# Two-layer convolution and attention kernel: the filters' stream pauses until its PSUM bank is copied out, and one column product is copied by VectorE

## The chip, the core and the metric

The kernel runs on one core of a Trainium2 chip. The metric is the time of one execution on the device in microseconds; lower is better. The engines are named as the profile names them: PE is TensorE (matmuls; PEld are its weight loads), DVE is VectorE, ACT is ScalarE, POOL is GpSimd, SP is SyncE, which here only issues DMAs. All data are fp32; an fp32 matmul appears in the trace as two records, so "x4" records of one product are two matmuls.

## The reference

The input x is 4 images of 256 channels and 48 x 48 pixels. Two layers follow each other, each added to its input. The first is a 3x3 convolution with batch norm, relu and self-attention with 8 heads; the second predicts, for each pixel, softmax weights for five 3x3 filters of growing dilation, applies them, mixes the six results with a 1x1 convolution, and normalizes over the batch.

```python
def layer0(g):                      # g = group norm of x, 32 groups
    h = relu(batch_norm(conv3x3(g, conv_w) + conv_b))
    q, k, v = qkv_w @ h + qkv_b     # 8 heads of 32 channels, 2304 pixels
    attn = softmax(q.T @ k * 32 ** -0.5)
    return proj_w @ (v @ attn.T) + proj_b

def layer1(g):                      # g = group norm of x + layer0
    guidance = conv3x3(g, W_cat)    # 45 channels = 5 filters x 9 taps
    outs = [g]
    for i, d in enumerate((1, 6, 12, 24, 36)):
        w = softmax(guidance[:, 9 * i : 9 * (i + 1)], axis=1)
        outs.append(sum_over_taps(shift(g, tap * d) * w[:, tap]))
    y = conv1x1(concat(outs), W_scale)
    return batch_norm_over_the_batch(y) * gamma + beta

x = x + layer0(group_norm(x))
x = x + layer1(group_norm(x))
```

## The kernel before

**Stages.** The images go through in a pipeline. Attention of image b runs alone (the function `attention`). Between two attentions lies a joint stage: the convolution and the q, k, v products of image b (`conv_qkv`, and in it `conv_blocks` for images 1 to 3) run together with the second layer of image b-1 (`dynamic_filters`). There are three joint stages, for `dynamic_filters` of b = 0, 1 and 2; a fourth and last run of `dynamic_filters` (b = 3, called `alone` in the code) has no convolution beside it. In the code, `b < B - 2` with B = 4 therefore means the first two joint stages.

**How the order is made.** Every engine executes its instructions in the order in which the program emits them. That order is worked out while the kernel is built, by a small planner. `clock` holds a planned time for PE, DVE, ACT and POOL; `clock(engine, ns, after)` puts a piece of work on an engine's planned time. `dynamic_filters` consists of streams, Python generators: `loads` (the DMAs of the far weights), `far` (the four large dilations, as matmuls), `rest` (sums for the next image's convolution), `near` (the dilation 1), `filters` (the softmax weights) and `mixes` (the 1x1 convolution). A stream yields the planned time at which its next piece may be emitted, either as a number or as a function that is asked again. The function `drive` looks through the streams in that order, and the first whose time has come (not later than PE's planned time) emits its piece. Only where none is due does `drive` take a step of the other generator, the convolution and qkv, and that only if `need[0]` says that its inputs and its PSUM bank are free in the plan. If nothing is due at all, PE's planned time is moved on. When the streams are done, `run(1e9)` emits what is left of the other generator.

**The softmax weights.** `weights(cs)` makes the weights of one chunk or of a pair of chunks; a chunk is a sixth of the image, 384 columns. `filters` calls it for the sets (0,), (1,), (2, 3), (4, 5), and asks before each that its first chunk be at most two beyond the chunk that `mixes` is at. In `weights`, PE computes `pg` (line 1545; 36 records for one chunk, 72 for a pair), ACT and DVE copy it to `lg` (1555, 1556), PE transposes it to `pt`, DVE and ACT make the softmax in `e1`, PE transposes it back to `pw` (1599), ACT copies `pw` to `lg` (1603), and SP stores `lg` to `w_d` in DRAM (1606). `pg`, `pt` and `pw` are all made by `misc`, which hands out the same PSUM bank each time: the next `pg` must wait until `pw` has been copied. The far weights `wq` are read back from `w_d` (1635) and meet PE in `wT` (1723); the near weights `ws` are read from it too (1802).

**The convolution of the joint stages.** `conv_blocks` works through 12 tiles, `t` from 0 to 11: six combinations of input rows, in the order 1, 2, 3, 4, 0, 5, with two halves of the output channels each. A tile consists of four column products, n = 0 to 3, of 288 columns each (`pc`, line 1176), which go round through two PSUM banks. The product n = 0 is copied to `one` (1191), the product n = 1 is combined with `one` into the two sums `two` (1201 and 1202), and the products 2 and 3 are added to them (1212 and 1214). Where the plan finds DVE late (`busy_dve`), ACT copies the products first (1196, 1207) and DVE or POOL adds.

**The start of a joint stage.** The last chunk of image b-1 is projected, its group norm is finished, and its 2 x 1152 columns in two halves of the image are normalized, half h = 0 of the channels by DVE (648) and h = 1 by ACT (2114). Between these pieces `run` emits convolution steps by their planned length: `run(2500)` and `run(1000)` during the norm's statistics, `run(1900)` after the first half of the image is normalized, `run(1400)` after the second. Tile t = 1 begins there: its n = 0 copy is emitted between the two halves of the normalization.

Of the kernel before, what the change touches and what calls it, by code (L numbers as in the profile page):

```python
# [15 lines left out]
B, C, HH, WW = 4, 256, 48, 48  # L16
# [42 lines left out]
def conv_preact_kernel(  # L59
# [12 lines left out]
    nc = tc.nc  # L72
# [480 lines left out]
    with tc.tile_pool(name="w", bufs=1) as wpool, tc.tile_pool(  # L553
# [60 lines left out]
        one = wpool.tile([P, 1], F32, tag="one", name="one")  # L614
# [20 lines left out]
        for j in range(2):  # L635
            t = act.tile([P, NH, PADW * PADW], F32, tag=f"pad{j}", name=f"pad{j}")
            t = t.rearrange("p h (r w) -> p h r w", w=PADW)
# [6 lines left out]
        def rows_of(t):  # L644
            return t.rearrange("p (r w) -> p r w", w=WW)
# [96 lines left out]
        clock = Clock()  # L742
        free = {}

        def slot(tag, bufs):

            ends = free.setdefault(tag, [])
            return ends[-bufs] if len(ends) >= bufs else 0.0
# [238 lines left out]
        class Blocks:  # L987
# [81 lines left out]
            def axpy(self, out, x, a, y):  # L1069
                if len(x.shape) == 4:  # L1070
                    for h in range(NH):
                        self.axpy(out[:, h], x[:, h], a, y[:, h])
                    return
                nc.vector.scalar_tensor_tensor(
                    out=out, in0=x, scalar=a, in1=y, op0=ALU.mult, op1=ALU.add
                )
# [31 lines left out]
        def conv_blocks(b, psum_tile, blocks, pool, hid):  # L1108

            axpy = blocks.axpy  # L1110
            tt = nc.vector.tensor_tensor
            rows = hid.rearrange("p h (t r w) -> p h t r w", r=4, w=WW)
            spare = list(blocks.spare)

            results, last = [], [0.0]

            def busy_dve():
                return clock.t["DVE"] > max(clock.t["ACT"], clock.t["PE"]) + 500

            def relu(o, r, y, end):  # L1120
                results.append((o, r, y, end))

            def relus(limit):
                while results and results[0][3] + 150 <= limit:
                    o, r, y, end = results.pop(0)
                    nc.scalar.activation(  # L1126
                        rows[:, o, :, r, :], rows_of(y), AF.Relu,
                        bias=bn_t[:, o : o + 1], scale=bn_s12[:, o : o + 1],
                    )
                    clock("ACT", 660, end)  # L1130

            def before(i, o):

                s12, d12, s34, d34 = (blocks.held[:, j, o] for j in range(4))
                if i == 0:
                    t = spare.pop(0)
                    axpy(t, s34, -4.0, s12)
                    relu(o, 2, t, clock.both(800))
                    either(s12, s12, s34, ALU.subtract)
                elif i == 5:  # L1140
                    t = spare.pop(0)
                    axpy(t, d34, -2.0, d12)
                    relu(o, 1, t, clock.both(800))
                    axpy(d12, d34, -8.0, d12)
                    clock.both(800)

            def target(i, o):

                if i in (1, 3):
                    return blocks.first[o]  # L1150
                if i in (2, 4):
                    return blocks.held[:, 1 if i == 2 else 3, o]
                return spare.pop(0)

            def after(i, o, y):

                s12, d12, s34, d34 = (blocks.held[:, j, o] for j in range(4))
                if i in (2, 4):
                    s, d = (s12, d12) if i == 2 else (s34, d34)
                    either(s, y, blocks.first[o], ALU.add)  # L1160
                    either(d, blocks.first[o], y, ALU.subtract)
                elif i in (0, 5):
                    relu(o, i and 3, y, either(y, y, s12 if i == 0 else d12, ALU.add))

            blocks.scaled()
            need[0] = lambda: 150 + max(slot("c", 2), blocks.end[STEPS[0]])
            for t, (i, o) in enumerate(TILES):
                u = us.pop(t)
                y = target(i, o).rearrange("p (n s) -> p n s", s=2)
                for n, j in enumerate((1, 2, 0, 3)):  # L1170
                    m = psum_tile(f"pc_{b}_{i}_{o}_{j}")[:, :XN]
                    clock("PE", 0, slot("c", 2), blocks.end[i, j])
                    z = blocks.of[i].rearrange("p (j h n) -> p j h n", j=4, h=NH)[:, j]
                    relus(max(clock.t["ACT"], clock.t["PE"]))
                    for h in range(NH):
                        nc.tensor.matmul(
                            m, u[:, h, j], z[:, h], start=(h == 0), stop=(h == NH - 1)
                        )
                        clock("PE", MM * XN / CH)
                        if h == 0:  # L1180
                            need[0] = lambda: 0.0
                            if t == 1 and n == 3:
                                blocks.along(ORDER[1])
                            if n == 0:
                                if t + 2 < len(TILES):
                                    us[t + 2] = taken(t + 2)
                                before(i, o)
                            yield MM * XN / CH
                    if n == 0:
                        one = pool.tile([P, XN], F32, tag="one", name=f"one_{b}_{i}_{o}")  # L1190
                        nc.scalar.copy(one, m)
                        end = clock("ACT", 400, clock.t["PE"])
                    elif n == 1:
                        two = pool.tile([P, 2, XN], F32, tag="two", name=f"two_{b}_{i}_{o}")
                        if busy_dve():
                            nc.scalar.copy(two[:, 1], m)
                            end = clock("ACT", 400, clock.t["PE"])
                            either(two[:, 0], one, two[:, 1], ALU.add, end)
                            either(two[:, 1], one, two[:, 1], ALU.subtract, end)
                        else:  # L1200
                            tt(two[:, 0], m, one, ALU.add)
                            tt(two[:, 1], one, m, ALU.subtract)
                            end = clock("DVE", 900, clock.t["PE"], end)
                    else:
                        to = y[:, :, n - 2]
                        if busy_dve():
                            nc.scalar.mul(to, m, 1.0 if j == 0 else -1.0)
                            end = clock("ACT", 450, clock.t["PE"])
                            either(to, to, two[:, n - 2], ALU.add, end)
                        else:  # L1210
                            if j == 0:
                                tt(to, m, two[:, 0], ALU.add)
                            else:
                                tt(to, two[:, 1], m, ALU.subtract)
                            end = clock("DVE", 480, clock.t["PE"])
                        if n == 3:
                            after(i, o, y.rearrange("p n s -> p (n s)"))
                    free["c"].append(end)
                    then = STEPS[4 * t + n + 1] if 4 * t + n + 1 < len(STEPS) else None
                    need[0] = lambda: 150 + max(  # L1220
                        slot("c", 2), blocks.end.get(then, NEVER) if then else last[0],
                    )
                    if n == 3 and o == NH - 1:
                        blocks.passed.add(i)
                    if then is None:
                        relus(NEVER)
                        last[0] = clock.t["ACT"]
                    yield MM * XN / CH
# [253 lines left out]
        def dynamic_filters(b, ao, chunk, norm, other, pools):  # L1482
# [48 lines left out]
            def weights(cs):  # L1531
# [72 lines left out]
                end = clock("ACT", 510, clock.t["PE"])  # L1604
                for s in range(len(cs)):
                    nc.sync.dma_start(
                        out=w_d[c + s, :, MARGIN : MARGIN + CH], in_=lg[64 * s : 64 * s + NG]
                    )
                    stored[c + s] = end + 2300

            def filters(sets):

# [497 lines left out]
            for part in range(2):  # L2110
                for h in range(NH):
                    t = inside(gn, h, HH // 2 * part, HH // 2)
# [267 lines left out]
        for b in range(B + 1):  # L2380

            with tc.tile_pool(name=f"work1_{b}", bufs=2) as work1, tc.tile_pool(
# [104 lines left out]
                else:  # L2487
                    if b == B:
# [18 lines left out]
                        t = wqkv.rearrange("p h k c -> p (h k c)")  # L2507
# [81 lines left out]
            with tc.tile_pool(name=f"work0_{b}", bufs=2) as work0, tc.tile_pool(  # L2589
# [4 lines left out]
                    lambda c, ao, pp, b=b, n=norm1: project(b, c, ao, pp, n), scratch, following,  # L2594
# [76 lines left out]
```

## Time and profile before

| | us |
|---|---|
| median of 3 runs | 2675.72 |
| lowest, highest | 2675.06, 2680.87 |
| the profiled execution | 2675.02 |
| its span, first to last instruction | 2673.2 |
| attention of image 1, about 798 to 1166 us from the start | 368 |
| joint stage 1, about 519 to 798 | 279 |
| joint stage 2, about 1166 to 1444 | 278 |
| joint stage 3, about 1814 to 2066 | 252 |
| the last run of the filters and the end, about 2440 to 2673 | 233 |

The profile is of one execution. A page of it gives the busy time of each engine over the whole span; the same sums can be had for a stretch of the span. A list of waits says which engine stood idle for the instruction of which line, and what ended that: "PE pg L1545 <- ACT lg L1603" is PE waiting at line 1545 for the copy of line 1603. A timeline gives the instructions in order of time, neighbours of one line put together; its columns are start and length in us, engine, line, operation, output and inputs, the number of records, and in brackets the idle time before them with what ended it.

### The profile page before, as it was taken

How to read it: one execution, taken by the hardware profiler on the slowest of the kernel's cores; microseconds unless marked ns; L12 is line 12 of the kernel's file. 1: busy time of each engine (PE TensorE's matmuls, PEld its weight loads, DVE VectorE, ACT ScalarE, POOL GpSimd, SP SyncE). 2: the span in 40 equal slices, each digit the busy share in tenths (PEclk: the TensorE clock that was granted, in tenths of full speed). 3: DMA queues.
4: the chain of work that ended last, by engine and by line, in shares of the span. 5: the costliest groups of instructions: out<-in, count | busy, mean ns of one | idle time of the engine just before them, and what ended most of it. 6: DMA issues, size and time to landing. Idle time of an engine off the chain costs nothing. (4 is left out here: it accounts for less than half of the span.)

```text
span 2673.2 us, 42578 instructions
## 1 busy us (share of the span) xinstructions
PE 2586.6 (97%) x16952; PEld 1092.1 (41%) x16952; DVE 2080.8 (78%) x2045; ACT 1802.6 (67%) x2281; POOL 789.6 (30%) x885
## 2 busy tenths in 40 slices
PE   7999999999999999999999999999989999999996
PEld 5632222555562222355555222245546222235554
DVE  7768998858739898967764989895775889895676
ACT  4479898734449999854445998984444989884344
POOL 4201001286520011057750001007765000100453
PEclk9999999999999999999999999999999999999998
DMA  4815445323252445433324354452324544433456
GB/s 174 225 42 107 101 101 114 92 65 103 70 108 72 101 95 114 102 81 89 95 63 91 89 113 101 101 108 79 89 69 125 128 106 95 107 84 79 121 165 222
DMA packets 138094, 279.96 MB, mean 105 GB/s; under 512 B 58152, under 2 KB 98512, under 8 KB 136864
## 3 DMA queue, kind: packets, MB, share of 16 engines
q0 software_dynamic: 27408, 144.00, 23.1%
q1 hardware_dynamic: 110480, 133.17, 18.9%
q8 instruction: 135, 2.21, 0.3%
q14 instruction: 71, 0.58, 0.1%
HBM read 112.12 MB, written 36.04 MB: 55 GB/s over the span
## 5 line engine op out<-in xcount | busy, mean ns | idle before, releaser
L1390 DVE TENSOR_TENSOR acc<-acc,p 128x2048 f32<-128x2048 f32 (+1 forms) x568 | 1039.3, 1830 | 96.7 <-ACT p L1351 46.2
L1351 ACT ACTIVATE p<-se 128x1536 f32<-128x1536 f32 x648 | 938.7, 1449 | 0.0
L1340 PE MATMUL se<-q,k 32*128 32x512 f32 (+1 forms) x4320 | 737.0, 593 | 0.0
L1340 PE MATMUL so<-q,k 32*128 32x512 f32 (+1 forms) x1440 | 728.3, 593 | 3.5 <-DVE bound L1295 2.0
L1375 PE MATMUL num<-p,vT 128*32 128x512 f32 (+1 forms) x5760 | 699.4, 561 | 1.7 <-ACT ao L1400 1.7
L1350 ACT ACTIVATE p<-so 128x512 f32<-128x512 f32 x648 | 388.5, 600 | 158.7 <-PE se L1340 63.1
L1340 PEld LDWEIGHTS so<-q,k 32*128 32x128 f32 x1440 | 216.5, 183 | 517.8 <-ACT p L1350 477.0
L1843 POOL TENSOR_TENSOR near<-near,prod 128x384 f32<-128x384 f32 x352 | 352.6, 1034 | 225.9 <-DVE prod L1837 222.8
L1394 POOL DMA_DIRECT2D ring<-p x128 | 109.1, 852 | 796.2 <-ACT p L1351 615.7
L1375 PEld LDWEIGHTS num<-p,vT 128*32 128x32 f32 x5760 | 129.0, 108 | 475.4 <-issue 448.9
L1837 DVE TENSOR_TENSOR prod<-wb,pad 128x768 f32<-128x768 f32 x192 | 182.1, 954 | 86.4 <-ACT wb L1824 53.1
L1340 PEld LDWEIGHTS se<-q,k 32*128 32x128 f32 x4320 | 227.1, 183 | 5.1 <-ACT p L1351 4.3
L1824 ACT COPY wb<-ws 128x384 f32<-128x384 f32 x216 | 108.7, 507 | 171.9 <-DVE prod L1837 127.9
L1392 POOL DMA_DIRECT2D ring<-p x36 | 20.1, 558 | 574.5 <-DVE ao L1428 274.1
L2001 PE MATMUL py<-far,wsc 128*128 128x384 f32 x512 | 169.9, 487 | 0.0
L1545 PE MATMUL pg<-pad,wcat 128*45 128x384 f32 x864 | 146.7, 490 | 8.8 <-ACT lg L1603 8.8
L1256 PE MATMUL pq<-hid,wqkv 128*128 128x384 f32 x384 | 133.9, 503 | 15.0 <-ACT hid L1126 12.8
L1513 ACT COPY far<-far 128x512 f32<-128x512 f32 x86 | 90.3, 1108 | 79.8 <-PE far L1771 76.4
L2001 PEld LDWEIGHTS py<-far,wsc 128*128 128x128 f32 x512 | 96.2, 190 | 66.0 <-issue 1.8
L1256 PEld LDWEIGHTS pq<-hid,wqkv 128*128 128x128 f32 x384 | 73.5, 195 | 69.6 <-ACT hid L1126 15.1
L1390 DVE TENSOR_TENSOR acc<-p,p 128x2048 f32<-128x2048 f32 x36 | 82.3, 2285 | 21.3 <-ACT p L1351 14.8
L1745 DVE COPY_PREDICATED amat<-along_y,bmat 128x768 f32<-128x768 uint32 x72 | 93.1, 1293 | 2.4
(336 smaller groups left out, 2836.7 us busy)
## 6 DMA issues: line engine op xcount, KB each, us to landing
ring<-p POOLq DMA_DIRECT2D x164, 768.0 KB, 5.7
ws<-w_d SPq DMA_DIRECT2D x216, 192.0 KB
ring<-u_d SPq DMA_DIRECT2D x36, 512.0 KB
pad<-in_x SPq DMA_DIRECT2D x14, 1152.0 KB
xst<-in_x POOLq DMA_DIRECT2D x36, 192.0 KB, 3.6
x_d<-pad SPq DMA_DIRECT2D x36, 192.0 KB
u_d<-pad SPq DMA_DIRECT2D x12, 512.0 KB
y_d<-y SPq DMA_DIRECT2D x13, 384.0 KB
```

The lines of the kernel that those rows point to most:

```text
L1256: nc.tensor.matmul(pq[:, :CH], wqkv[:, i, s, g * P : (g + 1) * P], hid[:, i, cols], start=(i == 0), stop=(i == NH - 1),)
L1340: nc.tensor.matmul(dst[:, at : at + n], k_[r, g, m * P : (m + 1) * P], q[r, g, q0 : q0 + n], start=True, stop=True,)
L1350: nc.scalar.activation(p[:, 0, :], s1, AF.Exp, scale=QS)
L1351: nc.scalar.activation(p[:, 1:, :], s3, AF.Exp, scale=QS)
L1375: nc.tensor.matmul(st["num"][r, at : at + n], vT[:, m, g * P + j * D : g * P + (j + 1) * D], p[:, j, at : at + n], start=(m == 0 and not s ...
L1390: nc.vector.tensor_tensor(st["acc"][:, js], other[:, js], p[:, js], ALU.add)
L1394: nc.gpsimd.dma_start(out=extra, in_=p[:, 1:], accum_op=ALU.add)
L1545: nc.tensor.matmul(pg[64 * s : 64 * s + NG, :CH], wcat[:, ii, k, :], shifted(ii, cc, k // 3 - 1, k % 3 - 1), start=(i == 0 and k == 0), st ...
L1824: nc.scalar.copy(pw[:, :CH], fetched[c, k][0])
L1837: nc.vector.tensor_tensor(prod.rearrange("p h (r w) -> p h r w", w=WW), wb, src, ALU.mult)
L1843: nc.gpsimd.tensor_tensor(cat[:, h], cat[:, h], prod[:, h], ALU.add)
L2001: nc.tensor.matmul(py[c][:, o, :CH], wsc[:, n * NH + i, o * P : (o + 1) * P], rhs, start=(n == 0 and i == 0), stop=(n == order[-1] and i = ...
```

## The change

There are two edits. In `conv_blocks`, the n = 0 product of tile t = 1 is copied by DVE and no longer by ACT, in all three joint stages, and is put on DVE's planned time with 450 ns; all other tiles keep ACT. In `weights`, after the stores have been issued, the stream yields the planned end of the copy of `pw` plus 150 ns in the first two joint stages, so that the next set isn't begun before that time of the plan.

```diff
@@ -1188,8 +1188,12 @@
                             yield MM * XN / CH
                     if n == 0:
                         one = pool.tile([P, XN], F32, tag="one", name=f"one_{b}_{i}_{o}")
-                        nc.scalar.copy(one, m)
-                        end = clock("ACT", 400, clock.t["PE"])
+                        if t == 1:
+                            nc.vector.tensor_copy(one, m)
+                            end = clock("DVE", 450, clock.t["PE"])
+                        else:
+                            nc.scalar.copy(one, m)
+                            end = clock("ACT", 400, clock.t["PE"])
                     elif n == 1:
                         two = pool.tile([P, 2, XN], F32, tag="two", name=f"two_{b}_{i}_{o}")
                         if busy_dve():
@@ -1607,6 +1611,8 @@
                         out=w_d[c + s, :, MARGIN : MARGIN + CH], in_=lg[64 * s : 64 * s + NG]
                     )
                     stored[c + s] = end + 2300
+                if b < B - 2:
+                    yield end + 150
 
             def filters(sets):
 
```

## The prediction, made before the changed kernel was run

> **What bounds the kernel now.** I read the page first: TensorE is busy 97% of the span, so either it works or it is made to wait. The change touches only the three joint stages, in which the convolution and qkv of image b run beside the filters of image b-1, so I took the busy times by stage next.
>
> ```profile
> span 2673.2 us, 42578 instructions
> PE 2586.6 (97%) x16952; PEld 1092.1 (41%) x16952; DVE 2080.8 (78%) x2045; ACT 1802.6 (67%) x2281; POOL 789.6 (30%) x885
> ...
> core 0: us, PE busy (x) PEld busy (x) DVE busy (x) ACT busy (x) POOL busy (x), PEclk, DMA share, GB/s
> ...
> 519.00:798.00 279.00, 267.67 (x1163) 160.20 (x1162) 175.94 (x243) 112.30 (x203) 166.81 (x153) 0.99 0.36 89
> ...
> 1166.00:1444.00 278.00, 266.86 (x1153) 159.20 (x1153) 175.64 (x242) 111.64 (x201) 166.56 (x153) 0.99 0.37 89
> ...
> 1814.00:2092.00 278.00, 259.83 (x1218) 146.91 (x1216) 184.95 (x241) 128.68 (x221) 172.51 (x158) 0.98 0.38 102
> ```
>
> Read the second column against the first: PE is idle 11.3, 11.1 and some 18 us (the third window takes in some attention). VectorE has over 90 us free in each. So a joint stage lasts as long as PE's work plus PE's waits, and the list of PE's waits in the first stage says which:
>
> ```profile
> engine line waited for: us in total, times, longest us
> PE pq L1256 <- ACT hid L1126: 3.0, 1, 3.0
> PE pg L1545 <- ACT lg L1603: 2.3, 2, 1.4
> PE pc L1176 <- ACT one L1191: 2.0, 2, 1.3
> PE wT L1723 <- DMA wq<-w_d: 1.2, 2, 0.7
> ```
>
> The change aims at the second and third lines. The timeline of PE shows where they fall:
>
> ```profile
> 527.49 1.70 PE L1176 MATMUL pc<-cv_v,ring 128*128 128x288 f32 x6
> 530.49 2.21 PE L1176 MATMUL pc<-cv_v,ring 128*128 128x288 f32 x8 [1.30 <-ACT one L1191]
> ...
> 547.70 0.49 PE L1599 MATMUL pw<-ident,e 128*128 128x128 f32 x3
> 548.03 0.65 PE L1176 MATMUL pc<-hid,ring 128*128 128x288 f32 x2
> 549.61 6.08 PE L1545 MATMUL pg<-pad,wcat 128*45 128x384 f32 x36 [0.93 <-ACT lg L1603]
> ...
> 573.53 0.55 PE L1599 MATMUL pw<-ident,e 128*128 128x128 f32 x3 [0.30 <-DVE e L1595]
> 575.49 2.17 PE L1545 MATMUL pg<-pad,wcat 128*45 128x384 f32 x12 [1.41 <-ACT lg L1603]
> ```
>
> The second stage has the same three waits at 1.30, 1.20 and 1.39 us, the third at 1.30, 0.92 and 1.42. The last piece of the stage is pure convolution side: in stage one the last filter product on PE is at 761.7 us, then pq and pv run without a gap to 797.9. No filter chain sets the end; a microsecond taken from PE's waits is a microsecond off the stage, unless a later wait takes it back.
>
> [...] the product of `one` is complete near 528.1 us, but its copy starts only behind the normalization:
>
> ```profile
> 528.81 1.35 ACT L2114 ACTIVATE pad<-pad,gshift_n,grstd_n 128x1152 f32<-128x1152 f32 x1
> 530.06 0.38 ACT L1191 COPY one<-pc 128x288 f32<-128x288 f32 x1
> 530.34 1.35 ACT L2114 ACTIVATE pad<-pad,gshift_n,grstd_n 128x1152 f32<-128x1152 f32 x1
> ```
>
> [...] The filters' `misc` tile has one bank, and the waits on L1603 are what that costs.
>
> **The change part by part.**
>
> (1) Copy of `one` on VectorE for t == 1: three copies in the program, one at the start of each joint stage. The trace has no such copy there; the nearest rows are VectorE copies from PSUM:
>
> ```profile
> L1515 DVE COPY xT<-xb x6: 416/425/425, 578.5 to 2594.3; 128x256 f32<-128x256 f32 x6
> L1515 DVE COPY xT<-xa x4: 692/693/693, 535.4 to 2453.6; 128x512 f32<-128x512 f32 x4
> ```
>
> From 425 ns for 256 columns and 693 for 512, 288 columns take 425 + 32 x 1.05 = 458 ns (bounds 416 and the 561 of the 384-column copy at L1556). [...] In VectorE's order the copy follows the first half of the normalization (L648, 528.30 to 529.18, which is itself needed) and precedes the two ops of `two`. So it runs about 529.15 to 529.6, where ScalarE's ended at 530.44. PE's next group starts at 529.6 in place of 530.49. Its partner needs the bank that `two` frees: two VectorE ops in succession, at their spacing of 0.38 us, end at 530.45, and PE's first two pairs run until 530.65, so that is no wait. What waits behind the copy on VectorE is the second half of the normalization; it moves from 531.21 to about 530.35, earlier, since `two` itself no longer waits. On ScalarE the second half follows the first directly, ending 531.4 in place of 531.69. PE reaches pg at about 531.77, after both. Gain 0.86 us a stage, x3 = 2.6. GpSimd's gate op, which waits 4.1 us for the normalization, also comes earlier.
>
> (2) The pause after the store, in the first two stages. There are four sets; after the third, the stream is held anyway until mix 2 begins (pw at 601.55, next pg at 646.58), and after the fourth nothing follows. So two places a stage count. The stream yields until the planned end of the L1603 copy plus 150, and the planner hands PE to the other streams.
> First place (549 us): ScalarE's plan there is `one` 400 and then 510, so some 1.2 us after pw's successor, which is three convolution steps of 486 planned ns. They are to be had: the next products of that tile have inputs and banks. PE runs six pc records (about 1.8 us) in place of 0.93 idle. But the convolution steps come from behind pg, and the DMA'd wq is next: at 557.36 `wT` already waits 0.50 for it, 7.8 us after the lg copy ended. That landing doesn't move. PE would come to it with pg ended at 548.68 + 1.8 + 6.08 = 556.56, and wait 0.8. Net, six pc records instead of four are done by 557.36: 0.6 gained of 0.93. In stage two `wT` began at 1203.79 without a wait, 7.4 us after its copy; PE would be there at 1203.1 and wait up to 0.7, so of 1.20 I count the same two records, 0.6.
> Second place (574 us): the fourth input row of the convolution isn't made yet, so no pc step is open. But the far products of chunk 0 are (their copies on ScalarE end at 574.1), so the first far mixes, four py records of 1.4 us, and the transposes xa, xb can go ahead of pg. Stall 1.41 falls to some 0.2: gain 1.2, and 1.2 in stage two. Chunk 1's wq has about 9 us from copy to use there, so it takes nothing back.
> Sum of (2): 0.6 + 1.2 + 0.6 + 1.2 = 3.6; bounds zero (nothing to fill) and 4.9 (all four waits).
>
> (3) What moves: the filters of chunk 1 and of 2, 3 come 1 to 3 us later against the rest: their stores on SP, the ws loads, the near products. Near ends 33 us before the stage does, so that is covered; without the cover it would be those 1 to 3 us a stage. Every later decision of the planner (which engine copies, who goes first) can flip too, alike in both stages. I put that at zero, with bounds of -3 to +4 us a stage.
>
> **Sum.** 2.6 + 3.6 = 6.2 us. The profiled execution took 2675.02 us (span 2673.2 and 1.8 around it), so 2668.8; the median is 0.7 above it, so 2669.5 on that scale.
>
> **The rivals.**
> (A) The waits are only moved: the filled time is given back at the next DMA landing or bank. Part (1) alone stays: 2675.7 - 2.6 = 2673.1. For: wT's wait at 557.36 sits right behind. Against: the second place has no such wait.
> (B) The handover to qkv (pq waits 3.0 us for the last relu) grows to the 6.1 us that stage three shows, where little is left to put there: +3.1 x 2 cancels the gain, 2675.7.
> (C) It shrinks to nothing, as more work of other streams falls on it: another 2 x 3.0 us, 2663.5.
> (D) Slower: the new order puts the convolution's bank copies behind far and near copies on ScalarE. In stage one this happens once, at 641.83 us: 0.68 us for `one`. Eight of twelve tiles follow the first pause, with four bank copies each, 64 in the two stages; were one in three to wait so, 21 x 0.68 = 14.3, less 6.2: 2683.8. It decides from 17 such waits (11.6 us: the gain and the 5.35 below). For: the order is a greedy plan which knows only its own clock. Against: ScalarE is busy just 40% of the stage, and the plan keeps its load levelled.
> (E) The change doesn't do what it says: t == 1 is one tile and the pause is skipped where the stream is held; that is counted above.
>
> **How the numbers follow.** A measurement here can tell about 0.2%, 5.35 us, from no change. Forecast 0.52, own range 2667.5 to 2671.5 (of it 0.46 below 2670.4); A 0.12, B 0.08, C 0.15, D 0.13. Faster 0.46 + 0.15 = 0.61; within 0.2%: 0.06 + 0.12 + 0.08 = 0.26; slower 0.13. The range runs from C, 2663, to the lower part of D, 2679, and leaves out the rest of D and the far side of C.
>
> **What would show it.** Right: `one` at the start of a stage on VectorE at about 0.46 us, PE's wait before the next group some 0.4 us, no wait on L1603 over 0.3 us in the first two stages and the same 0.92 and 1.42 in the third; the two stages shorter by about 2.6 us each and the third by 0.9. Wrong: a longer wait of wT, of pq or of pc on ScalarE's copies, or PE idle in the first two stages at 11 us as before.

## The result, and the profile after

The changed kernel takes 2692.06 us (median of 5 runs, 2691.16 to 2696.71); the kernel before, timed beside it, takes 2679.75 (2675.06 to 2682.35). The ratio on record is 1.0060 (95% interval 1.0048 to 1.0071): 13 to 19 us slower, where 6.2 us faster was forecast. The two medians alone, of five runs each, lie 12.3 us apart (1.0046); two kernels below in which TensorE has the same order as in the changed one (the pause alone, and the copies issued early) come to 1.0055 and 1.0057. I call the loss 16 us in what follows.

The profiled execution of the changed kernel is the longest of its five, 2696.71 us, and that of the kernel before, 2675.02, is as short as the shortest of its five, so the two traces lie further apart than the medians do. The page of the changed kernel begins with:

```profile
span 2694.9 us, 42581 instructions
...
PE 2600.1 (96%) x16952; PEld 1100.6 (41%) x16952; DVE 2079.6 (77%) x2044; ACT 1807.5 (67%) x2288; POOL 786.3 (29%) x885
```

As many TensorE records as before are busy 13.5 us longer. To see where, I cut each joint stage at the same two events, the first matmul of the stage and the first product after it. These are the busy times by stretch, first two stages of the kernel before, then of the changed kernel (columns as in the prediction's table: stretch, length, busy time of PE, PEld, DVE, ACT and POOL with their instructions, granted clock, DMA share, GB/s):

```profile
516.69:797.89 281.20, 269.87 (x1173) 161.91 (x1171) 177.79 (x247) 114.42 (x204) 169.04 (x155) 0.99 0.36 89
1163.31:1445.61 282.30, 271.11 (x1174) 162.62 (x1172) 177.87 (x247) 114.53 (x204) 169.18 (x155) 0.99 0.37 88
```

```profile
514.95:809.11 294.16, 278.47 (x1173) 167.03 (x1171) 177.32 (x246) 117.15 (x208) 166.94 (x155) 0.96 0.35 85
1174.50:1468.00 293.50, 278.22 (x1174) 167.25 (x1172) 177.04 (x246) 117.22 (x208) 167.76 (x155) 0.96 0.35 85
```

The stages are 13.0 and 11.2 us longer. Length less PE's busy time is its idle time: 11.33 and 11.19 us before, 15.69 and 15.28 after, so 4.4 and 4.1 us more. The rest, 8.6 and 7.1 us, is more busy time for the same 1173 and 1174 records: the clock column fell from 0.99 to 0.96. The third stage has 255.45 before and 255.04 after, the attentions between the stages and the end agree within 0.3 us, and the time ahead of the first stage, where nothing was changed, is 1.7 us shorter. The loss lies in the two stages that have the pause. Their waits, changed kernel, first stage (engine, line, what ended the wait; total us, times, longest):

```profile
PE wT L1729 <- DMA wq<-w_d: 7.3, 3, 3.3
PE far L1777 <- DVE amat L1751: 2.1, 1, 2.1
PE xa L1699 <- ACT lg L1607: 1.3, 1, 1.3
PE xa L1699 <- DVE own L1519: 1.2, 1, 1.2
```

The three waits the change aimed at have gone, but for 0.4 us behind the copy of `one`, and so has the 3.0 us wait of pq. In their place PE waits for the read-back of the far weights, 1.2 us before and 7.3 now, and once for `amat`, which VectorE makes out of wT.

The place where it turns is the first pause. The prediction shows PE before up to pg; behind pg, the kernel before goes on with:

```profile
555.62 1.24 PE L1176 MATMUL pc<-hid,ring 128*128 128x288 f32 x4
557.36 0.88 PE L1723 MATMUL wT<-ident,wq 36*64 36x36 f32 x12 [0.50 <-DMA wq<-w_d]
558.16 0.87 PE L1568 MATMUL pt<-pick,lg 128*128 128x45 f32 x6
```

PE in the changed kernel, in order of time (start, length, then as in the prediction's timeline):

```profile
545.05 0.49 PE L1603 MATMUL pw<-ident,e 128*128 128x128 f32 x3
545.38 2.11 PE L1176 MATMUL pc<-hid,ring 128*128 128x288 f32 x8
547.41 6.09 PE L1549 MATMUL pg<-pad,wcat 128*45 128x384 f32 x36
555.66 0.88 PE L1729 MATMUL wT<-ident,wq 36*64 36x36 f32 x12 [2.17 <-DMA wq<-w_d]
556.47 4.63 PE L1176 MATMUL pc<-hid,ring 128*128 128x288 f32 x18
563.17 1.13 PE L1777 MATMUL far<-amat,xT 64*128 64x256 f32 x8 [2.07 <-DVE amat L1751]
564.24 0.87 PE L1572 MATMUL pt<-pick,lg 128*128 128x45 f32 x6
```

The pause does what the forecast said: eight pc records in place of two after pw, and pg without a wait. But wT then waits 2.17 us, and starts 555.66 - 514.95 = 40.71 us into the stage; before it was 557.36 - 516.69 = 40.67. What was won by then, 0.9 us at the start and as much at the pause, has been handed back, but for two pc records (eight stand between pw and wT, before it was two and four), some 0.6 us. And pt, which stood directly behind wT before, now comes after the far product, 49.3 us into the stage and not 41.5. The order in which the pieces were emitted can be seen on VectorE, whose 2045 instructions before and 2044 after stand in the two traces, by their lines, in the order of the program. The copy of pg to `lg`, which pt reads, and its neighbours, before and then after:

```profile
556.28 0.56 DVE L1556 COPY lg<-pg 45x384 f32<-45x384 f32 x1 [7.08 <-ACT lg L1555]
...
558.27 1.51 DVE L1733 COPY_PREDICATED bmat<-along_x,wT 128x288 f32<-128x288 uint32 x3 [0.56 <-PE wT L1723]
559.81 4.62 DVE L1745 COPY_PREDICATED amat<-along_y,bmat 128x768 f32<-128x768 uint32 x3
```

```profile
556.58 1.52 DVE L1739 COPY_PREDICATED bmat<-along_x,wT 128x288 f32<-128x288 uint32 x3 [8.16 <-PE wT L1729]
558.13 4.99 DVE L1751 COPY_PREDICATED amat<-along_y,bmat 128x768 f32<-128x768 uint32 x3
563.15 0.56 DVE L1560 COPY lg<-pg 45x384 f32<-45x384 f32 x1
```

The planner emits the last pg products, yields once more, and only then emits the copies. In the kernel before, wT fell due in the plan a little after that point (less than 1.0 us of the plan, as `early_wt` below shows). With the pause wT is due by then, and wT, `bmat` and `amat` go first. That was my first theory of the loss, and it did not hold in this form.

The busy time shows in slices of 2 us behind these two waits, changed kernel (columns as above):

```profile
564.00:566.00 2.00, 1.63 (x11) 1.21 (x8) 1.48 (x2) 1.67 (x2) 2.00 (x2) 0.89 0.00 0
566.00:568.00 2.00, 2.00 (x8) 1.17 (x6) 1.20 (x3) 2.00 (x4) 2.00 (x3) 0.50 0.06 21
568.00:570.00 2.00, 2.00 (x5) 1.17 (x4) 1.75 (x3) 1.20 (x2) 1.14 (x1) 0.50 0.27 78
570.00:572.00 2.00, 2.00 (x6) 1.35 (x4) 0.95 (x2) 0.62 (x2) 1.54 (x2) 0.50 0.63 123
572.00:574.00 2.00, 2.00 (x12) 1.09 (x11) 0.31 (x1) 0.75 (x2) 2.00 (x3) 0.91 0.59 238
```

The granted clock (third column from the right) stands at one half for some 6.8 us, with PE busy all the time: eight pc records take 4.15 us there and 2.21 elsewhere. The half clock follows waits of 2.17 and 2.07 us with 5.4 us of work between them.

In the traces of both kernels, the times at which the granted clock changes lie whole multiples of 3.4133 us apart, to within 1 ns. I took the idle time of PE between each two such points. The 2.17 us wait of wT lies across one of them, with 1.80 us ahead of 555.30 and 0.36 behind. How much idle time between two points goes with a fall of the clock, the traces don't settle: in the changed kernel the half clock followed 1.41 us (562.13 to 565.54) and did not follow 1.80 us (551.89 to 555.30). Where more than 2 us at the full clock were idle, it followed each time, in 11 cases in the two traces.

### The profile page after: what moved, and what is told of

Its sections match the earlier page's. It is cut to its first block, busy times and chain, and to the rows that moved or that the text cites. A ratio compares the mean times of both kernels' runs of the same rounds, so it can differ in the third digit from the quotient of the medians.

```text
span 2694.9 us, 42581 instructions
## 1 busy us (share of the span) xinstructions
PE 2600.1 (96%) x16952; PEld 1100.6 (41%) x16952; DVE 2079.6 (77%) x2044; ACT 1807.5 (67%) x2288; POOL 786.3 (29%) x885
## 3 DMA queue, kind: packets, MB, share of 16 engines
q1 hardware_dynamic: 110480, 133.17, 18.7%
q8 instruction: 135, 2.21, 0.3%
```

## The experiments

All times are the ratio to the kernel before, timed on the same chip; "+5 us" means the ratio less one times 2677 us. The letters used in the expectations: theory O, the flipped order around wT and the `lg` copies is the loss; theory C, the lower clock after waits is a large part of it. The others are said where they stand.

### The parts alone

Each keeps a part of the change and drops the rest. `one_only` drops the pause, `pause_only` drops the copy on VectorE, and two kernels keep one of the two places of the pause:

```diff
-                if b < B - 2:
+                if b < B - 2 and c == 0:
                     yield end + 150
```

(`pause_first`; `pause_second` has c == 1; both without the copy on VectorE.)

> Only the copy of `one` for t == 1 moves to VectorE; no pause. Theory P (the pause before the second set costs everything): the three joint stages each lose about 0.4 to 0.9 us of PE's 1.30 us wait, so 1.2 to 2.6 us faster than before. Rival Q (VectorE's copy delays the start of the stage and carries on): 4 us or more slower than before.

Measured: 0.9981 (0.9975 to 0.9988), -5.1 us.

> Only the pause; `one` stays on ScalarE. The order of PE is that of the changed kernel. Theory P: 17 to 19 us slower than before in the two first stages together, some 1 to 2 us slower than the changed kernel. Rival Q: less than 10 us slower than before.

Measured: 1.0055 (1.0039 to 1.0071), +14.7 us.

> Only the pause after set (0,), in the first two joint stages. Theory P1 (the first pause shifts the second set against the landing of wq, so that wT is emitted before the copies of pg, and VectorE's copy of pg then waits behind wT's DMA and 6.5 us of predicated copies): slower than before by 10 us or more, wT waits over 5 us a stage. Rival P2 (the second pause does it): within 4 us of before.

Measured: 1.0039 (1.0027 to 1.0051), +10.4 us.

> Only the pause after set (1,), in the first two joint stages. Theory P1: the order after it is nearly that of before, the wait of 1.4 us for the copy of pw goes to some 0.2 in both stages: 2 to 2.5 us faster than before. Rival P2: slower than before by 10 us or more.

Measured: 0.9988 (0.9980 to 0.9996), -3.2 us.

So the copy on VectorE is a gain, the second place of the pause is a gain, and the first place turns it all round. The parts don't add up: -5.1, +10.4 and -3.2 make +2, and the whole is +16. With the first place in the kernel, neither of the other two gains anything that can be seen (+10.4 alone, +14.7 with the second place, +16.1 with both). The copy and the second place together, the change without the first place:

> The copy of `one` on VectorE, and the pause after set (1,) alone, in the first two joint stages: the two parts that were faster by themselves, by 5.1 and 3.2 us. If their gains add up: 7 to 9 us faster than before. If both only remove the same waits: 4 to 6 us.

Measured: 0.9978 (0.9968 to 0.9988), -5.9 us (-8.6 to -3.2), which can't tell the two cases of the expectation apart. For these two parts the forecast has 2.6 + 2.4 = 5.0.

### The order put back

The yield behind the last products of a single set goes, so that the copies of pg are emitted at once:

```diff
-                    if at + 3 < 9 * NH:
+                    if at + (3 if pair else 6) < 9 * NH:
                         yield 0.0
```

> The changed kernel, but the single sets don't yield after their last group of pg, so that the copies of pg are emitted ahead of wT, as in the kernel before. Theory O (the order on VectorE is what the loss hangs on: its copy of pg stands behind bmat and amat, and those behind wT's DMA): at least half of the loss of 16 us comes back, 2678 to 2686 us; pt of set (1,) comes some 7 us earlier in the stage. Rival W (what counts is that PE reaches wT before its data): less than 4 us come back.

Measured: 0.9960 (0.9947 to 0.9973), 2664.1 us, -10.7 us; faster than both kernels. PE in this kernel, at the same place:

```profile
547.43 6.08 PE L1549 MATMUL pg<-pad,wcat 128*45 128x384 f32 x36
555.11 0.87 PE L1729 MATMUL wT<-ident,wq 36*64 36x36 f32 x12 [1.59 <-DMA wq<-w_d]
555.91 0.86 PE L1572 MATMUL pt<-pick,lg 128*128 128x45 f32 x6
```

With the same two pauses, wT still waits 1.59 us. So the wait that I had priced at 0.8 is not the loss in itself. pt is behind wT again, and the stage goes on undisturbed: 276.20 us, of which 8.16 idle, clock 1.00. The pause is not what costs; what the plan makes of it is. The kernel before with the yield taken out and no pause was not run, so how much of the 27 us between the two kernels is the undone turn, and how much the missing yield would gain by itself, is not shown.

### The clock

Idle matmuls, whose results are overwritten unread, stand ahead of wT of chunks 0 to 2 and of the first far product of chunk 0. They take the place of waiting and shorten no wait:

```diff
                     wq = wqs.pop(c).rearrange("k (m b) -> k b m", b=STEP)
+                    if b < B - 2 and c < 3:
+                        busy(bank, (4, 3, 6)[c])
...
                         clock("PE", 0, slot("k", banks_k - 1))
+                        if b < B - 2 and c == p == 0:
+                            busy(two[0], 4)
```

> The changed kernel with matmuls of no use in front of wT (4, 3 and 6 of them for chunks 0, 1 and 2) and 4 in front of the first far product, in the first two joint stages, where PE stood idle 1.8 to 3.6 us. Nothing is ready earlier. Theory C (of the loss, more than half is the lower granted clock after those waits): 6 us or more faster than the changed kernel, the granted clock of the two stages back at 0.98 or 0.99. Rival I (the idle time itself is the loss): within 3 us of the changed kernel.

Measured: 1.0019 (1.0010 to 1.0028), +5.1 us. Some 11 of the 16 us come back with the order unchanged and the clock at 1.00 and 0.99 in the two stages. In its trace the two stages are still 3.5 and 4.2 us longer than before, near the 4.4 and 4.1 us of added idle time. Not all 11 us are the price of the waits that were filled: in the trace of the changed kernel the clock is also at one half for 6.83 us from 719.14 on, behind waits of 0.36, 0.36, 0.46 and 0.70 us that no idle matmul fills. They stand in this kernel as well, for 0.36, 0.35, 0.46 and 0.70 us, and here the clock stays up. The same with chunk 0 alone:

> The changed kernel with idle matmuls, 4 ahead of wT and 4 ahead of the first far product, of chunk 0 alone in the first two stages; all else as in the changed kernel. Theory C (two waits of some 2 us within 10 us bring the granted clock down): the slice of 0.66 after them is 0.95 or more, and 3 to 7 us of the 16 come back (2684 to 2689 where the changed kernel stands at 2692). Rival (the clock falls by something else, or each wait counts by itself): within 2 us of the changed kernel.

Measured: 1.0055 (1.0038 to 1.0072), +14.7 us: nothing that can be told from the changed kernel, against theory C's number. Of the changed kernel's slices of 10 us, the one of 0.66 after that pair did rise to 1.00, but slices of 0.83, 0.83 and 0.66 remain later in the first stage. One pair's price is not shown.

The same idea in the kernel before, with 4 idle matmuls ahead of the first q product in stages 1 and 2 and 10 in stage 3:

```diff
                         end = clock("PE", 2 * MM, slot("c", 2))
+                        if b and c == g == s == 0:
+                            busy(pq, 10 if b == B - 1 else 4)
```

> The kernel before with idle matmuls ahead of the first q product of each joint stage, 4 in the first two stages and 10 in the third, where TensorE waits 3.0 and 6.1 us for the last relu; nothing else moves. Theory C (a wait costs its length and a lower granted clock after it): faster by 2 to 5 us (2671 to 2674), and the granted clock after the third-stage wait near 1. Rival (a wait costs its length only): within 1.5 us of before.

Measured: 0.9981 (0.9973 to 0.9989), -5.1 us, with no work removed. The kernel before had paid for its pq waits by the clock as well: its half-clock stretches there, 3.41 and 6.83 us in the first two stages, are gone, and the mean granted clock over the span is 0.995, against 0.992. In the third stage the expectation fails: with 2.9 us of the wait left, the clock still falls to one half behind it, for 3.41 us where it was 6.83.

### What in the order costs

First a blunt test: the planned landing of every wq 3 us later.

```diff
-                    landed[c] = clock.t["PE"] + 2600
+                    landed[c] = clock.t["PE"] + (5600 if b < B - 2 else 2600)
```

> The changed kernel, but the planner is told that wq lands 5.6 us after its issue and no longer 2.6 (the trace shows about 4.9 from the first issue, and the issue itself late) in the first two joint stages. Theory O and W alike: wT is emitted when its data are there, its waits fall from 7 to under 2 us a stage, and 10 us or more of the loss come back. Rival R (any other order than that of before loses): slower than before by 8 us or more.

Measured: 1.0138 (1.0122 to 1.0153), +37 us. It came out as neither O nor W had it; rival R's number is met, but R itself (any other order loses) falls with `copies_first`. In its first stage the waits of wT are gone, and these lead the list instead:

```profile
PE pc L1176 <- ACT wb L1830: 9.9, 1, 9.9
PE pc L1176 <- POOL hid L1094: 5.4, 1, 5.4
```

Moving all six chunks moves the whole plan; it tells nothing of the cause. Then two kernels for the late copy. The first is the kernel before with the copies of chunk 1 held back, the second the changed kernel with the copies ahead on VectorE and ScalarE, but TensorE's order kept to the instruction:

```diff
+                if b < B - 2 and c == 1: yield clock.t["PE"] + 600
                 nc.scalar.copy(lg[:NG, :], pg[:NG, :CH])
```

> The kernel before, with neither of the two edits; only the copies of pg to lg of the second set (chunk 1) are held back 600 planned ns in the first two stages, so that wT and VectorE's bmat and amat of chunk 0 are emitted ahead of them, the order that the changed kernel has. Theory O (the flipped order of the lg copies against wT, bmat and amat is the loss): slower than the kernel before by 8 to 16 us (2684 to 2692), with waits at wT of 5 us or more in each of the first two stages, and pt of chunk 1 some 7 us later in the stage than before. Rival P (the pause itself costs, by holding the filters back, whatever the order of the copies): within 4 us of before, since the stream is held 0.6 us only.

Measured: 0.9997 (0.9989 to 1.0006), no change. Theory O falls in the form "late copies cost". pt comes 48.6 us into the stage, as late as in the changed kernel, and nothing is lost.

```diff
                     clock("PE", 3 * MM)
+                    if at + (3 if pair else 6) >= 9 * NH:
+                        nc.scalar.copy(lg[:NG, :], pg[:NG, :CH])
+                        nc.vector.tensor_copy(lg[64 : 64 + NG, :], pg[64 : 64 + NG, :CH])
...
-                nc.scalar.copy(lg[:NG, :], pg[:NG, :CH])
-                nc.vector.tensor_copy(lg[64 : 64 + NG, :], pg[64 : 64 + NG, :CH])
                 yield 150 + max(
```

> The changed kernel with the copies of pg to lg issued together with the last pg products of every set, while the plan and so TensorE's order stay word for word as in the changed kernel: on VectorE the lg copy then stands ahead of bmat and amat. Theory Q (VectorE's real queue is the loss: the lg copy stands behind copies that wait for a DMA): lg copy some 7 us earlier, and 8 us or more of the 16 come back (2676 to 2684). Rival R (TensorE's own order is the loss: the transposes pt stand behind wT and the far products in the plan, however early lg is there): within 5 us of the changed kernel (2687 to 2694).

Measured: 1.0057 (1.0042 to 1.0073), +15.3 us. Its `lg` copy runs at 556.47 and the loss is all there: VectorE's place for the `lg` copy is not the cause. PE's order, record for record that of the changed kernel in both stages, is what is left, with the plan that made it. Its two stages, by stretch:

```profile
517.28:803.09 285.81, 271.76 (x1174) 163.84 (x1171) 179.29 (x246) 117.21 (x208) 168.09 (x155) 0.99 0.35 87
1168.46:1460.73 292.27, 278.42 (x1173) 166.91 (x1171) 177.81 (x246) 117.18 (x208) 166.18 (x155) 0.96 0.34 85
```

One plan, and nearly the same idle time, 14.05 and 13.85 us; yet 6.5 us between them, all of it busy time at 0.99 and 0.96. This is a share of the clock, seen inside one execution.

Then the opposite of the pause: the kernel before with wT of chunk 0 planned 1.0 us earlier, and no pause at all.

```diff
-                    landed[c] = clock.t["PE"] + 2600
+                    landed[c] = clock.t["PE"] + (1600 if b < B - 2 and c == 0 else 2600)
```

> The kernel before with neither edit; only the planned landing of chunk 0's wq is 1.0 us earlier in the first two stages (1600 in place of 2600), so that wT follows pg at once, without the four convolution records between, and pt comes behind the first far product, as in the changed kernel. Theory F (TensorE at wT and amat before their data, with the work that used to cover this spent elsewhere): waits of about 1.7 us at wT and 2 us at the far product, a lower granted clock after them, and 8 us or more slower than before (2686 to 2695), without any pause. Rival S (the loss needs the pause, which spends convolution work ahead of pg): within 5 us of before, as with the copies held back alone.

Measured: 1.0056 (1.0039 to 1.0073), +15.0 us. The whole size of the loss, without the pause. Compare PE in the harmless kernel with the copies held back and then in this one:

```profile
551.11 6.09 PE L1544 MATMUL pg<-pad,wcat 128*45 128x384 f32 x36 [0.93 <-ACT lg L1603]
557.12 1.24 PE L1176 MATMUL pc<-hid,ring 128*128 128x288 f32 x4
558.86 0.88 PE L1723 MATMUL wT<-ident,wq 36*64 36x36 f32 x12 [0.50 <-DMA wq<-w_d]
559.67 6.09 PE L1176 MATMUL pc<-hid,ring 128*128 128x288 f32 x24
565.69 1.13 PE L1771 MATMUL far<-amat,xT 64*128 64x256 f32 x8
```

```profile
549.48 6.12 PE L1545 MATMUL pg<-pad,wcat 128*45 128x384 f32 x36 [0.93 <-ACT lg L1603]
557.22 0.88 PE L1723 MATMUL wT<-ident,wq 36*64 36x36 f32 x12 [1.62 <-DMA wq<-w_d]
558.03 5.60 PE L1176 MATMUL pc<-hid,ring 128*128 128x288 f32 x22
563.75 1.13 PE L1771 MATMUL far<-amat,xT 64*128 64x256 f32 x8
```

In both, pt follows the far product. They part first at one thing, whether four pc records stand ahead of wT or behind it, and end 16 us apart. At wT itself that is worth 1.1 us. The rest follows later in the plan, where the two orders part at more places, and not as it does in the changed kernel:

```profile
PE pq L1256 <- ACT hid L1126: 5.1, 1, 5.1
PE wT L1723 <- DMA wq<-w_d: 2.8, 2, 1.6
PE pg L1545 <- ACT lg L1603: 2.3, 2, 1.4
PE far L1771 <- DVE amat L1745: 1.9, 2, 1.0
PE pc L1176 <- DVE two L1202: 1.9, 2, 1.5
```

Here the stage is 8.8 us longer than before and has 18.71 us of idle time, 7.4 more, at a clock of 0.99: the loss is nearly all waiting, spread over pq (2.1 us more), wT, far and pc (some 1.5 more each). So theory F's time was met and its path was not.

Last, the changed kernel with wT of chunk 0 planned 2.0 us later, once with the copies still behind wT, `bmat` and `amat` (the line of `copies_late` added) and once without:

```diff
-                    landed[c] = clock.t["PE"] + 2600
+                    landed[c] = clock.t["PE"] + (4600 if b < B - 2 and c == 0 else 2600)
```

> The changed kernel with the planned landing of chunk 0's wq 2.0 us later in the first two stages and the lg copies of chunk 1 still behind bmat and amat: two convolution records go ahead of wT, pt stays behind the first far product as in the changed kernel. Theory F: the waits at wT and at the far product of chunk 0 fall by 1 us or more in sum, and 8 us or more of the 16 come back (2684 or less). Rival T (the late softmax chain of chunk 1 together with the pause is the loss): 2686 or more, with wT of chunks 1 and 2 still waiting 1.5 us or more each.

Measured: 1.0019 (1.0012 to 1.0026), +5.1 us: 11 us come back with the late copies left as they are; wT of chunk 0 waits 0.76. Theory F's number is met. Still the waiting at this place didn't simply go: a pc product just behind wT now stands 2.65 us, for nothing that the profile shows. The gain is in the stage as a whole, whose idle time is 12.04 and 11.03 us in the two stages, against 15.69 and 15.28.

> The changed kernel with the planned landing of chunk 0's wq 2.0 us later in the first two stages: the lg copies come ahead of wT, bmat and amat again, and two convolution records ahead of wT. Theories F and T both: the loss is gone, 2662 to 2674. If it is still 2680 or more, both are wrong, and the pause costs by something else.

Measured: 1.0032 (1.0020 to 1.0043), +8.6 us. Here both theories failed. wT of chunk 0 has no wait, but pt now stands where it waits 2.45 us for `lg`, and a pc product waits 3.0 us for VectorE's sums.

### Further with the order put back

> The changed kernel with the copies ahead of the other streams, and the pause in the third joint stage too. With the copies ahead, theory O has the pause free of its side effect: as fast as copies first with the pause in two stages, or up to 3 us faster (2661 to 2665), as the third stage's two waits of 0.92 and 1.42 us go. Rival: the third stage's planned order turns otherwise, and it is 3 us or more slower than that kernel.

Measured: 0.9967 (0.9953 to 0.9981), with the pause in three stages (b < B - 1): the third stage is 259.39 us in its trace, against 256.92 with the copies first and the pause in two stages. The traces lean to the rival, but that one is of the longest of five executions and the other of the shortest, and the ratios (0.9967 and 0.9960) can't be told apart.

> The kernel with the copies first and the pause in two stages, with 10 idle matmuls ahead of the first q product of the third stage, where TensorE waits 6.1 us for the last relu. Theory C: 2 to 4 us faster than the kernel with the copies first alone (2660 to 2662 against 2664), since the clock after that wait stays up. Rival: same as that kernel within 1 us.

Measured: 0.9964 (0.9953 to 0.9975), with the third stage's 10 idle matmuls added to the kernel with the copies first: no gain over that kernel's 0.9960. The version with the copies first has the lowest ratio, though not clear of these two.

## Why the prediction was wrong

**What bounds the kernel** held: a joint stage is PE's work plus PE's waits, and the change acts only there. What it left out is that PE's work has no fixed length. The clock at which it runs changes with the waits: the same 1173 and 1174 records took 8.6 and 7.1 us more at 0.96 than at 0.99, and with idle matmuls in the waits (`warm_wt`) the clock stood at 1.00 and 0.99.

**Part (1), the copy of `one`,** was right. PE and the copy in the changed kernel:

```profile
527.86 2.21 PE L1176 MATMUL pc<-cv_v,ring 128*128 128x288 f32 x8 [0.41 <-DVE one L1192]
...
530.00 2.16 PE L1549 MATMUL pg<-pad,wcat 128*45 128x384 f32 x12
```

```profile
L1192 DVE COPY one<-pc x3: 450/450/451, 527.4 to 1845.8; 128x288 f32<-128x288 f32 x3
```

0.450 us against 0.458 forecast; a wait of 0.41 against 0.4; pg 15.05 us into the stage against 15.94, so 0.89 gained against 0.86. Alone it was timed at -5.1 us (-6.7 to -3.2) against -2.6. What the rest comes from was not settled; the trace of that kernel, of one of its longer executions (2676.76 us), doesn't show it.

**Part (2), second place,** was right in size: -3.2 us (-5.4 to -1.1) against -2.4, taken alone. "So it takes nothing back" did not hold in the changed kernel, where wT of chunk 1 waits 1.80 and 1.59 us in the two stages.

**Part (2), first place,** failed by its wT term. The count came true: "six pc records instead of four" are two more, and eight against six stand ahead of wT. "That landing doesn't move" came true as well: wT starts 40.7 us into the stage in both kernels. What failed is the wait, "0.8", which is 2.17. It was reckoned for a TensorE that part (1) brings no earlier (0.89 us), and with 1.8 us for six pc records, which took some 1.4. So the two gains that the sum adds, 0.86 and 0.6, run into the same landing, and of both together some 0.6 is left. Why the landing stays: the stores went out 1.0 us earlier in the stage and the reads did not. From the store of `lg` to the first read of it, SP in the changed kernel and then in the kernel before:

```profile
546.92 0.40 SPq L1610 DMA_DIRECT2D w_d<-lg  x1
550.71 3.12 SPq L1641 DMA_DIRECT2D wq<-w_d  x4
```

```profile
549.63 0.40 SPq L1606 DMA_DIRECT2D w_d<-lg  x1
552.43 3.10 SPq L1635 DMA_DIRECT2D wq<-w_d  x4
```

3.79 us against 2.80, with no other issue in between. Why the read came so much later behind the store stays open.

**Part (3) is the step that the forecast failed by.** "Every later decision of the planner ... can flip too, alike in both stages. I put that at zero, with bounds of -3 to +4 us a stage." In the traces the two stages are 13.0 and 11.2 us longer, with all that parts (1) and (2) gained already in it. Of this 4.4 and 4.1 us are waiting, at the read-back of the far weights above all (7.3 us in place of 1.2 in the first stage), and 8.6 and 7.1 are the same work at a lower clock, which the prediction has no term for. The sentence also says "covered" of filters that come 1 to 3 us later. They came 8 us later at chunk 1 and 13 at chunks 2 and 3 (pw 65.2 and 98.4 us into the stage, 56.8 and 84.9 before), and the read-back of chunk 2 waited 3.3. The prediction names no ground in the profile for its bounds; neighbouring plans range from 7.7 us of idle time in a first or second stage (the copies first) to 18.7 (the early wT) and 26.5 (every landing moved).

**The rivals.** Rival A, the wait handed on to the next DMA landing, is what happened at the first place, but it ends at the gain of part (1) alone and has no loss in it. C's step came true as well, pq's wait is gone from both stages, and it was outweighed. D, the slower case, named the wrong engine: of PE's waits for the convolution's bank copies on ScalarE, the list of the first stage has two, of 0.7 and 0.4 us, where D needed 17 in the two stages. Its sentence "a greedy plan which knows only its own clock" was the right ground, with a mechanism of the wrong kind.

**Shown, and left open.** Shown: the first place of the pause makes the loss; the order behind it, not the waiting time of the pause, carries it (copies first, and the early wT with no pause); the late `lg` copy alone and its place on VectorE are not it; the clock is the larger part of the loss in this kernel (some 11 of 16 us came back with idle matmuls, 15.7 of 24.2 us in the traces are busy time), though not in the early wT, which loses as much by waiting. Open: by which chain a wT four records too early becomes 4 to 7 us of waiting a stage. It took different ways in different plans.

## What to carry to other kernels

In a kernel whose order comes from a greedy plan, price an edit to the plan by its nearest decision points: look which other piece is due within a microsecond of the place, what stands behind it, and keep wide bounds on both sides if one is. Take the edit apart by place; here two of three parts gained 5.9 us and the third lost more than that. Waits on TensorE can cost more than their length, by the clock after them: here 8.6 and 7.1 us of slower work came with 4.4 and 4.1 us of added waiting. Where they can't be removed, try idle matmuls in their place: they brought 11 and 5 us in two kernels here, and nothing in two others.

## What the runs showed of the hardware

In the joint stages of the kernel before, the granted clock of TensorE went to 0.50 once a stage, for 3.41, 6.83 and 6.83 us; in those of the changed kernel four times in each of the first two, for 6.83, 3.41, 6.83 and 6.83 us, and once in the third, for 6.83. In the changed kernel's first stage this followed waits of 1.80 to 3.31 us, and once only waits of 0.36 to 0.70 us close together. How far the mean clock fell differed with the same order and nearly the same idle time: two stages of one kernel (`copies_early`), with 14.05 and 13.85 us of it, ran at 0.99 and 0.96, 6.5 us apart. Filling waits of the kernel before with idle matmuls, without any other change, gained 5.1 us (2.9 to 7.2). The two traces differ by 15.7 us in PE's busy time of the first two stages, for the same number of records.
